# Pairing the TensorE bursts and state updates of a Mamba2 block: products of two units in one piece

## The chip, the cores and the metric

The kernel runs on one core of one Trainium2 chip. The metric is the device time of one launch in microseconds (us); lower is better. All data is float32. The four compute engines run their own instruction streams side by side: TensorE (PE, with its weight loads listed apart as PEld), VectorE (DVE), ScalarE (ACT) and GpSimd (POOL). The SP queue issues most of the DMAs. [...]

## The reference

One adaptive-layer-norm block over 4 sequences of 512 tokens with 512 features. A layer norm, scaled and shifted by values that come from a conditioning vector, goes through a Mamba2 mixer and is added back with a gate; then a second such layer norm goes through one matrix of signs (times a row mean) with a bias, again with a gate. The part that the change touches is the chunked scan of the mixer:

```python
    Y_diag = jnp.einsum('bcshn,bczhn,bhcsz,bczhp->bcshp', Cm, Bm, Lm, X)
    decay_states = jnp.exp(A_cum[..., -1:] - A_cum)
    states = jnp.einsum('bcshn,bhcs,bcshp->bchpn', Bm, decay_states, X)
    ...
    new_states = jnp.einsum('bhzc,bchpn->bzhpn', decay_chunk, states)
    states = new_states[:, :-1]
    state_decay_out = jnp.exp(A_cum)
    Y_off = jnp.einsum('bcshn,bchpn,bhcs->bcshp', Cm, states, state_decay_out)
```

There are 64 heads with 16 values each, in 8 groups that share B and C with 64 state entries, and chunks of 128 tokens. `Y_diag` needs, for each group, the product of B and C over the state entries (128 x 128, masked and multiplied by the decays of each head). `Y_off` needs the product of C with the state that came in from the chunk before. The new state is the old one, decayed, plus a product of B with the decayed inputs.

## The kernel before

The 2048 tokens are worked in 8 halves of 256 tokens (`NHALF`), two to a sequence, and each half in 2 chunks of 128. A **unit** is one chunk and one pair of groups: (h, c, gp) with gp from 0 to 3, so there are 8 x 2 x 4 = 64 units. For each half a "front" makes the layer norm, the projections (`pp_B`, `pp_C`, `pp_x`, `pp_z`, line 433), the convolution on ACT and DVE (lines 446 and 450), the turned copies (`pt_bt`, `pt_xt`) and the sums of the time steps. Behind each chunk come three "tails": the output projection (`po`, line 722), the second layer norm (`ph`, line 740) and the last matrix (`pf`, line 758).

The order is written by hand. Lists (`FIRST`, `SECOND`, `FRONT`, lines 770 to 793) give each piece of a front a step; the loop from line 828 runs the steps from -1. Step s runs the pieces due at s, then `burst`, then `stage2` of unit s, then `stage0` and `stage1` of unit s + 2. This text order is the priority: a compile-time scheduler places each engine's instructions by it as soon as they look ready and a buffer is free, so a piece that is held up lets later ones pass. `glued` (line 208) keeps products of one piece next to each other on TensorE.

- `burst(old, new)` (lines 594 to 608) issues up to four products into one PSUM tile `gy` with one buffer [...]: the state outputs of unit s (C times state, two products, one for each half of the rows) and the B times C products of unit s + 2 (again two). These are 64 rows deep, so the two of a pair lie on different halves of the array. Units of the first chunk of a sequence have no state coming in, and their bursts lack the first pair.
- `stage1` reads B times C out of `gy` on DVE, masked, into `gm` (line 619), runs 16 exponentials on ACT in place over `decay` tiles that a DMA has filled with broadcast sums (line 545), and multiplies both with two DVE instructions (line 623).
- `stage2` multiplies the decays with the inputs on TensorE into `py` (two glued pieces of eight products, output 32 partitions wide, lines 647 to 655), reads the state output from `gy` on DVE (line 664), adds `py` (669), and on POOL adds `xs` and multiplies by `z` (670, 673). Then, except in the last chunk of a sequence, it makes the new state of its pair of groups: POOL makes `xd` (line 680, two buffers), TensorE two products into a PSUM tile `pst` (line 685, 64 columns wide), POOL decays the old state into the new tile (line 690), and DVE adds `pst` (line 695); in the first chunk DVE copies `pst` instead (line 688). `pst` is one of the tiles of the tag `mm`, which has five buffers [...] and also serves all projections, turns and tails.

TensorE's products in float32 appear as two matmul records each in the trace. So a full burst has 8 records, `pst` of one unit 4, `py` of one unit 32.

Of the kernel before, what the change touches and what calls it, by code (L numbers as in the profile page):

```python
# [11 lines left out]
F32 = mybir.dt.float32  # L12
AF = mybir.ActivationFunctionType
ALU = mybir.AluOpType
AX = mybir.AxisListType
PSUM = bass.MemoryType.PSUM
P = 128

B, L, DM = 4, 512, 512
DI, NS, NG, NH = 1024, 64, 8, 64  # L20
HD = DI // NH
# [4 lines left out]
CH = 128  # L26
T = 256
NHALF = B * L // T
HPB = L // T
# [10 lines left out]
def adaln_mamba_block(  # L40
# [15 lines left out]
    nc = tc.nc  # L56
    mm = nc.tensor.matmul

    def bc(ap, n):

        return ap.unsqueeze(2).to_broadcast([ap.shape[0], ap.shape[1], n])

    def bc_mid(ap, n):

        return ap.unsqueeze(1).to_broadcast([ap.shape[0], n, ap.shape[1]])
# [3 lines left out]
    ps = ctx.enter_context(tc.tile_pool(name="ps", bufs=5, space=PSUM))  # L69
    wk = ctx.enter_context(tc.tile_pool(name="wk", bufs=2))  # L70
# [22 lines left out]
    upto = keep.tile([P, P], F32, name="upto")  # L93
# [114 lines left out]
    def glued(products, after=None):  # L208

        with tc.issue_after(after) if after else nullcontext():  # L210
            first = products[0]()  # L211
        with tc.issue_after(first.ins), tc.high_priority(offset=1000):
            for product in products[1:]:
                product()  # L214
# [89 lines left out]
    H = [dict(B={}, C={}, xt={}, xs={}, bt={}, z={}) for _ in range(NHALF)]  # L304
# [217 lines left out]
    NP = NG // 2  # L522
    HPP = 2 * HPG
    states = {}
    U0, U1, G = {}, {}, {}
    n_decay = [0]

    def is_first(h, c):
        return h % HPB == 0 and c == 0
# [10 lines left out]
    def exps(h, c, gp, ets):  # L540
        hd0 = c * NH + gp * HPP
        for r in range(2):
            for i in range(HPG):
                hd = hd0 + r * HPG + i
                nc.scalar.activation(  # L545
                    ets[r][:, i, :], ets[r][:, i, :], AF.Exp, bias=H[h]["st"][:, hd : hd + 1], scale=-1.0
                )
# [18 lines left out]
    def stage0(h, c, gp):  # L566

        n = f"{h}_{c}_{gp}"
        ets = AHEAD.get((h, c, gp))
        if ets is None:  # L570
            ets = own_decays()
            load_sums(h, c, gp, ets)
        e = None
        if not is_first(h, c):
            e = wk.tile([P, 2, CH], F32, tag="e", name=f"e_{n}")
            for r in range(2):
                lo = (2 * gp + r) * HPG
                nc.sync.dma_start(
                    e[:, r, :],
                    e_d[h, c, lo : lo + HPG, :].unsqueeze(1).to_broadcast([HPG, HD, CH]),  # L580
                )
        U0[h, c, gp] = (ets, e)

    def by_rows(gy, slot, h, c, gp, stationary):

        return [
            partial(
                mm, gy[:, r, slot, :], stationary[part],
                H[h]["C"][gp // 2][part, gp % 2, c * CH : (c + 1) * CH], start=True, stop=True,
            )  # L590
            for r, part in enumerate((slice(0, NS), slice(NS, P)))
        ]

    def burst(old, new):

        gy = ps.tile([P, 2, 4, CH], F32, tag="gy", bufs=1, name="gy_" + "_".join(map(str, old or new)))
        products = []
        if old is not None:
            h, c, gp = old
            k = (h % HPB) * 2 + c  # L600
            if k > 0:
                products += by_rows(gy, 1, h, c, gp, states[h // HPB, k][:, gp, :])
                G[old, 1] = gy
        if new is not None:
            h, c, gp = new
            products += by_rows(gy, 0, h, c, gp, H[h]["B"][gp // 2][:, gp % 2, c * CH : (c + 1) * CH])
            G[new, 0] = gy
        glued(products)

    def stage1(h, c, gp):  # L610

        n = f"{h}_{c}_{gp}"
        ets, e = U0.pop((h, c, gp))
        gm = wk.tile([P, 2, CH], F32, tag="gm", name=f"gm_{n}", bufs=3)
        nc.vector.tensor_mul(gm, G.pop(((h, c, gp), 0))[:, :, 0, :], bc_mid(upto, 2))
        if (h, c, gp) not in AHEAD:  # L620
            exps(h, c, gp, ets)
        for r in range(2):
            nc.vector.scalar_tensor_tensor(  # L623
                ets[r], ets[r], 1.0, bc_mid(gm[:, r, :], HPG), ALU.min, ALU.mult
            )
        U1[h, c, gp] = (ets, e)

    def stage2(h, c, gp):

        n = f"{h}_{c}_{gp}"
        k = (h % HPB) * 2 + c
        b = h // HPB
        ets, e = U1.pop((h, c, gp))
        hd0 = c * NH + gp * HPP
        xp = H[h]["xt"][gp][:, c, :]
        xg = xp.rearrange("p (j q e) -> p j q e", q=4, e=HD)[:, :, 0:4:3, :]

        def by_head(v):

            return v.rearrange("p (j q) -> p j q", q=2).unsqueeze(3).to_broadcast([P, HPG, 2, HD])

        py = ps.tile([P, 2, CH], F32, tag="y", bufs=1, name=f"py_{n}")

        for r in range(2):
            glued([
                partial(
                    mm, py[32 * j : 32 * j + 32, r, :],  # L650
                    xp[:, r * 2 * P + 32 * (2 * j + q) : r * 2 * P + 32 * (2 * j + q) + 32],
                    ets[r][:, 2 * j + q, :], start=(q == 0), stop=(q == 1),
                )
                for q in range(2) for j in range(HPG // 2)
            ], H[1]["last"] if (h, c) == (0, 1) else None)

        cs = slice(c * CH, (c + 1) * CH)
        zg = H[h]["z"][gp][:, :, cs]
        xs = H[h]["xs"][gp][:, :, cs]
        t = wk.tile([P, 2, CH], F32, tag="gm", name=f"yt_{n}", bufs=3)  # L660

        ew = nc.vector if h == NHALF - 1 and c == 1 and gp >= NP // 2 else nc.gpsimd
        if k > 0:
            nc.vector.tensor_mul(t, G.pop(((h, c, gp), 1))[:, :, 1, :], e)
            if ew is nc.vector:
                ew.tensor_add(t, t, xs)
                ew.tensor_add(t, py, t)
            else:
                nc.vector.tensor_add(t, py, t)  # L669
                ew.tensor_add(t, t, xs)  # L670
        else:
            nc.vector.tensor_add(t, py, xs)  # L672
        ew.tensor_mul(zg, t, zg)  # L673

        if k < HPB * 2 - 1:
            if gp == 0:
                states[b, k + 1] = wk.tile([P, NP, P], F32, tag="S", name=f"S_{b}_{k + 1}")
            new = states[b, k + 1][:, gp, :]
            xd = wk.tile([P, HPG, 2, HD], F32, tag="xd", name=f"xd_{n}")
            nc.gpsimd.tensor_tensor(xd, xg, by_head(H[h]["ed"][:, hd0 : hd0 + HPP]), ALU.mult)  # L680
            xd2 = xd.rearrange("p j q e -> p (j q e)")
            pst = ps.tile([P, P], F32, tag="mm", name=f"pst_{n}")
            bt = H[h]["bt"][gp // 2][:, c, gp % 2, :]
            for r in range(2):
                mm(pst[r * NS : (r + 1) * NS, :], bt[:, r * NS : (r + 1) * NS], xd2[:, r * P : (r + 1) * P],  # L685
                   start=True, stop=True)
            if k == 0:
                nc.vector.tensor_copy(new, pst)
            else:
                nc.gpsimd.tensor_tensor(  # L690
                    new.rearrange("p (h e) -> p h e", e=HD),
                    states[b, k][:, gp, :].rearrange("p (h e) -> p h e", e=HD),
                    bc(H[h]["dec"][:, c * NP + gp, :], HD), ALU.mult,
                )
                nc.vector.tensor_add(new, new, pst)


    gates = {}
# [124 lines left out]
    h = NHALF - 1  # L823
# [3 lines left out]
    units = [(h, c, gp) for h in range(NHALF) for c in range(2) for gp in range(NP)]  # L827
    for step in range(-1, max(steps) + 1):
        for f, args in steps.get(step, []):
            f(*args)  # L830

        new = units[step + 2 : step + 3] if step >= 0 else units[0:2]
        if step < 0:
            for unit in new:
                burst(None, unit)
                stage0(*unit)
                stage1(*unit)
        elif step < len(units):
            if new or not is_first(*units[step][:2]):
                burst(units[step], new[0] if new else None)  # L840
            stage2(*units[step])
            for unit in POST.get(step, []):
                ahead(*unit)
            for unit in new:
                stage0(*unit)
                stage1(*unit)
# [42 lines left out]
```

## Time and profile before

| what | value |
|---|---|
| median of 3 runs | 748.45 us (746.47 to 752.62) |
| the profiled execution | 747.6 us |
| its span, first to last instruction | 745.9 us |
| TensorE busy | 711.2 us, 5196 matmul records |
| VectorE busy | 602.6 us, 1218 instructions |
| ScalarE busy | 523.7 us, 1507 instructions |
| GpSimd busy | 260.4 us, 313 instructions |
| `gy` matmul records | 448, of them 192 of states |
| `pst` matmul records | 192 |
| `py` matmul records | 2048 |

Times within the trace count from the first instruction. Matmuls are pipelined: the time that one record is said to take (about 0.27 us for a moving side of 128) is much longer than the time from its start to the start of the next, so the cost of a piece on TensorE is read from start to start, and a busy TensorE isn't one at its peak. In the group rows a name such as `gy<-C,S` says which tile is written from which; `128*64` behind a matmul is the part of the array it uses, rows times columns.

### The profile page before, as it was taken

The numbers are of one execution on the slowest core, as the hardware profiler recorded it, in microseconds if no ns is written. First come the engines' busy times: TensorE is split into PE (matmuls) and PEld (weight loads), VectorE is DVE, ScalarE is ACT, GpSimd is POOL, SyncE is SP. The second block draws the span as 40 slices with busy tenths as digits, with TensorE's granted clock in tenths as the row PEclk, the third lists the DMA queues.
The fourth block names the chain that finished last, engine by engine and source line by source line (L and its number), as shares of the span: only waits on it lengthen the run. The fifth ranks groups of instructions, "written<-read, shape, count | busy, mean of one in ns | idle before, by whom it ended". The sixth has DMA issues, their size and how long they took to land.

```text
span 745.9 us, 15107 instructions
## 1 busy us (share of the span) xinstructions
PE 711.2 (95%) x5196; PEld 503.2 (67%) x5196; DVE 602.6 (81%) x1218; ACT 523.7 (70%) x1507; POOL 260.4 (35%) x313
## 2 busy tenths in 40 slices
PE   6999979899999999999999999999999999999997
PEld 3787647566677666686667666876667866677654
DVE  3968889866999579986899769996699867997795
ACT  2476668648796596775877777764969658798941
POOL 4021325334242433353224243533324232343452
PEclk9999989899999999999999999999999999999999
DMA  8991865435654266434634246543544436458610
GB/s 280 317 289 39 237 164 121 113 86 138 125 146 125 63 158 140 106 101 99 158 101 119 75 108 165 149 110 69 139 125 121 129 79 175 104 152 167 143 58 28
DMA packets 119068, 99.25 MB, mean 133 GB/s; under 512 B 73984, under 2 KB 97152, under 8 KB 118992
## 3 DMA queue, kind: packets, MB, share of 16 engines
q1 hardware_dynamic: 117808, 96.39, 50.6%
q0 software_dynamic: 896, 1.38, 0.6%
q8 instruction: 41, 0.67, 0.4%
q10 hardware_dynamic: 288, 0.52, 0.2%
q14 instruction: 35, 0.29, 0.1%
HBM read 92.47 MB, written 5.79 MB: 132 GB/s over the span
## 4 chain that ended last, share of the span: by engine, by line
PE 77%; ACT 14%; DVE 5%; issue 2%; DMA 2%; ACTq 0%; POOL 0%; SPq 0%; DVEq 0%
PE pp_x L433 16%; PE po L722 15%; PE pp_z L433 12%; ACT decay L545 10%; PE pp_B L433 7%; PE pp_C L433 7%; PE pf L758 4%; PE py L211 3%; PE py L214 3%; PE gy L211 2%; PE pt_xt L463 2%; PE pst L685 2%; PE pa L367 1%; DMA decay<-sums_d 1%; ACT h L742 1%
## 5 line engine op out<-in xcount | busy, mean ns | idle before, releaser
L545 ACT ACTIVATE decay<-decay,st 128x128 f32<-128x128 f32 x960 | 293.0, 395 | 4.0 <-DMA decay<-sums_d 3.7
L623 DVE SCALAR_TENSOR_TENSOR decay<-decay,gm 128x1024 f32<-128x1024 f32 x120 | 156.8, 1308 | 25.1 <-ACT decay L545 24.1
L433 PE MATMUL pp_x<-hT,win 128*128 128x259 f32 x512 | 122.5, 394 | 5.8 <-ACT decay L545 5.8
L433 PE MATMUL pp_z<-hT,win 128*128 128x256 f32 x512 | 118.1, 383 | 0.0
L433 PEld LDWEIGHTS pp_x<-hT,win 128*128 128x128 f32 x512 | 98.0, 195 | 24.1 <-ACT decay L545 6.0
L722 PE MATMUL po<-wout,z 128*128 128x512 f32 x256 | 113.9, 595 | 0.0
L433 PEld LDWEIGHTS pp_z<-hT,win 128*128 128x128 f32 x512 | 94.3, 189 | 16.1 <-issue 3.3
L680 POOL TENSOR_TENSOR xd<-xpad,st 128x256 f32<-128x256 f32 x48 | 37.6, 784 | 188.3 <-PE pst L685 143.0
L450 DVE SCALAR_TENSOR_TENSOR u_x<-pp_x,cw,u_x 128x256 f32<-128x256 f32 x192 | 82.9, 473 | 1.4 <-ACT u_x L446 0.5
L722 PEld LDWEIGHTS po<-wout,z 128*128 128x128 f32 x256 | 47.4, 190 | 52.6 <-issue 51.7
L512 ACT ACTIVATE uz<-pp_z,zb 128x256 f32<-128x256 f32 x64 | 26.8, 468 | 62.3 <-PE pp_z L433 62.3
L670 POOL TENSOR_TENSOR yt<-yt,xs 128x256 f32<-128x256 f32 x46 | 41.1, 893 | 84.4 <-DVE yt L669 84.4
L214 PE MATMUL py<-decay,xpad 128*32 128x128 f32 x1680 | 67.4, 276 | 0.0
L673 POOL TENSOR_TENSOR z<-yt,z 128x256 f32<-128x256 f32 x62 | 58.5, 944 | 17.1 <-DVE yt L672 13.6
L433 PE MATMUL pp_B<-hT,win 128*128 128x259 f32 x256 | 60.9, 388 | 0.9 <-ACT st L426 0.9
L758 PE MATMUL pf<-bwT,h 128*128 128x512 f32 (+1 forms) x136 | 59.1, 575 | 0.8 <-ACT h L742 0.6
L433 PE MATMUL pp_C<-hT,win 128*128 128x259 f32 x256 | 59.0, 382 | 0.0
L503 POOL TENSOR_TENSOR xs<-u_x,rr 128x512 f32<-128x512 f32 x32 | 42.1, 1318 | 40.8 <-DVE u_x L455 40.8
L433 PEld LDWEIGHTS pp_B<-hT,win 128*128 128x128 f32 x256 | 47.0, 189 | 10.8 <-ACT st L426 1.7
L433 PEld LDWEIGHTS pp_C<-hT,win 128*128 128x128 f32 x256 | 47.8, 189 | 7.8 <-DVE u_B L450 0.3
L446 ACT ACTIVATE u_x<-pp_x,cb,cw 128x256 f32<-128x256 f32 x64 | 35.2, 559 | 25.1 <-PE pp_x L433 24.8
L211 PE MATMUL py<-decay,xpad 128*32 128x128 f32 x240 | 47.5, 280 | 3.8 <-ACT decay L545 2.8
(155 smaller groups left out, 1134.0 us busy)
## 6 DMA issues: line engine op xcount, KB each, us to landing
decay<-sums_d SPq DMA_DIRECT2D x120, 256.0 KB
decay<-sums_d SPq DMA_DIRECT2D x120, 128.0 KB
rr<-r_d SPq DMA_DIRECT2D x64, 128.0 KB
e<-e_d SPq DMA_DIRECT2D x96, 64.0 KB
win<-in_w_inT SPq DMA_DIRECT2D x4, 1024.0 KB
xr<-in_x SPq DMA_DIRECT2D x16, 256.0 KB
res<-o SPq DMA_DIRECT2D x15, 256.0 KB
x<-in_x SPq DMA_DIRECT2D x14, 256.0 KB
```

The lines of the kernel that those rows point to most:

```text
L211: first = products[0]()
L214: product()
L433: last = mm(pm, win[:, k, col : col + P], H[h]["hT"][:, k, lo:], start=(k == 0), stop=(k == NK - 1))
L450: nc.vector.scalar_tensor_tensor(u[:, j, :], pm[:, k : k + T], cw[:, t, k : k + 1], u[:, j, :], ALU.mult, ALU.add)
L503: nc.gpsimd.tensor_tensor(xs, xc, rr, ALU.mult)
L545: nc.scalar.activation(ets[r][:, i, :], ets[r][:, i, :], AF.Exp, bias=H[h]["st"][:, hd : hd + 1], scale=-1.0)
L623: nc.vector.scalar_tensor_tensor(ets[r], ets[r], 1.0, bc_mid(gm[:, r, :], HPG), ALU.min, ALU.mult)
L670: ew.tensor_add(t, t, xs)
L673: ew.tensor_mul(zg, t, zg)
L680: nc.gpsimd.tensor_tensor(xd, xg, by_head(H[h]["ed"][:, hd0 : hd0 + HPP]), ALU.mult)
L722: last_po = mm(po, H[h]["z"][g // 2][:, g % 2, c * CH : (c + 1) * CH], wout[:, g, :], start=(g == 0), stop=(g == NKI - 1))
L758: mm(pf, h2[:, k, :], bwT[:, k, cols], start=(k == 0), stop=(k == NK - 1))
```

## The change

`burst` now takes lists of units. It is called in even steps only, and makes the state outputs of units s and s + 1 and the B times C products of units s + 2 and s + 3: eight glued products into one `gy` tile, whose four slots are now all used. The tile keeps its size and its one buffer. The readers on DVE stay as they were, one read for each unit.

The new states move out of `stage2` into `new_states`, called in the second unit of each pair of units (odd gp). `xd` is still made by POOL for each unit, in its own step. The four products of both units are glued and go to one `pst` tile of 128 x 256; the decay on POOL and the add (or copy) on DVE become one instruction of 128 x 256 for two of 128 x 128.

```diff
     def burst(old, new):
-        gy = ps.tile([P, 2, 4, CH], F32, tag="gy", bufs=1, name="gy_" + "_".join(map(str, old or new)))
+        gy = ps.tile([P, 2, 4, CH], F32, tag="gy", bufs=1, name="gy_" + "_".join(map(str, (old or new)[0])))
         products = []
-        if old is not None:
-            h, c, gp = old
+        for i, (h, c, gp) in enumerate(old):
             k = (h % HPB) * 2 + c
             if k > 0:
-                products += by_rows(gy, 1, h, c, gp, states[h // HPB, k][:, gp, :])
-                G[old, 1] = gy
-        if new is not None:
-            h, c, gp = new
-            products += by_rows(gy, 0, h, c, gp, H[h]["B"][gp // 2][:, gp % 2, c * CH : (c + 1) * CH])
-            G[new, 0] = gy
+                products += by_rows(gy, 2 + i, h, c, gp, states[h // HPB, k][:, gp, :])
+                G[(h, c, gp), 1] = gy[:, :, 2 + i, :]
+        for i, (h, c, gp) in enumerate(new):
+            products += by_rows(gy, i, h, c, gp, H[h]["B"][gp // 2][:, gp % 2, c * CH : (c + 1) * CH])
+            G[(h, c, gp), 0] = gy[:, :, i, :]
         glued(products)
...
             xd = wk.tile([P, HPG, 2, HD], F32, tag="xd", name=f"xd_{n}")
             nc.gpsimd.tensor_tensor(xd, xg, by_head(H[h]["ed"][:, hd0 : hd0 + HPP]), ALU.mult)
-            xd2 = xd.rearrange("p j q e -> p (j q e)")
-            pst = ps.tile([P, P], F32, tag="mm", name=f"pst_{n}")
-            bt = H[h]["bt"][gp // 2][:, c, gp % 2, :]
-            for r in range(2):
-                mm(pst[r * NS : (r + 1) * NS, :], bt[:, r * NS : (r + 1) * NS], xd2[:, r * P : (r + 1) * P],
-                   start=True, stop=True)
...
+            XD[gp % 2] = xd.rearrange("p j q e -> p (j q e)")
+            if gp % 2:
+                new_states(h, c, gp - 1)
+
+    def new_states(h, c, gp):
...
+        both = slice(gp, gp + 2)
+        new = states[b, k + 1][:, both, :].rearrange("p g e -> p (g e)")
+        pst = ps.tile([P, 2, P], F32, tag="mm", name=f"pst_{h}_{c}_{gp}")
+        bt = H[h]["bt"][gp // 2]
+        glued([
+            partial(
+                mm, pst[r * NS : (r + 1) * NS, i, :], bt[:, c, i, r * NS : (r + 1) * NS],
+                XD[i][:, r * P : (r + 1) * P], start=True, stop=True,
+            )
+            for i in (1, 0) for r in range(2)
+        ])
+        pst = pst.rearrange("p g e -> p (g e)")
+        if k == 0:
+            nc.vector.tensor_copy(new, pst)
+        else:
+            nc.gpsimd.tensor_tensor(
+                new.rearrange("p (h e) -> p h e", e=HD),
+                states[b, k][:, both, :].rearrange("p g (h e) -> p (g h) e", e=HD),
+                bc(H[h]["dec"][:, c * NP + gp : c * NP + gp + 2, :].rearrange("p j h -> p (j h)"), HD), ALU.mult,
+            )
+            nc.vector.tensor_add(new, new, pst)
...
         if step < 0:
+            burst([], new)
             for unit in new:
-                burst(None, unit)
                 stage0(*unit)
                 stage1(*unit)
         elif step < len(units):
-            if new or not is_first(*units[step][:2]):
-                burst(units[step], new[0] if new else None)
+            if step % 2 == 0 and (step + 2 < len(units) or not is_first(*units[step][:2])):
+                burst(units[step : step + 2], units[step + 2 : step + 4])
             stage2(*units[step])
```

More of the change, by code (lines that the diff above doesn't have):

```diff
@@ L618, in stage1 @@
         gm = wk.tile([P, 2, CH], F32, tag="gm", name=f"gm_{n}", bufs=3)
-        nc.vector.tensor_mul(gm, G.pop(((h, c, gp), 0))[:, :, 0, :], bc_mid(upto, 2))
+        nc.vector.tensor_mul(gm, G.pop(((h, c, gp), 0)), bc_mid(upto, 2))
         if (h, c, gp) not in AHEAD:
@@ L663, in stage2 @@
         if k > 0:
-            nc.vector.tensor_mul(t, G.pop(((h, c, gp), 1))[:, :, 1, :], e)
+            nc.vector.tensor_mul(t, G.pop(((h, c, gp), 1)), e)
             if ew is nc.vector:
@@ L675, in stage2 @@
         if k < HPB * 2 - 1:
-            if gp == 0:
-                states[b, k + 1] = wk.tile([P, NP, P], F32, tag="S", name=f"S_{b}_{k + 1}")
-            new = states[b, k + 1][:, gp, :]
             xd = wk.tile([P, HPG, 2, HD], F32, tag="xd", name=f"xd_{n}")
             nc.gpsimd.tensor_tensor(xd, xg, by_head(H[h]["ed"][:, hd0 : hd0 + HPP]), ALU.mult)
-            xd2 = xd.rearrange("p j q e -> p (j q e)")
-            pst = ps.tile([P, P], F32, tag="mm", name=f"pst_{n}")
-            bt = H[h]["bt"][gp // 2][:, c, gp % 2, :]
@@ L684, in stage2 @@
-            for r in range(2):
-                mm(pst[r * NS : (r + 1) * NS, :], bt[:, r * NS : (r + 1) * NS], xd2[:, r * P : (r + 1) * P],
-                   start=True, stop=True)
[L687 to L695, printed above, removed]
+            XD[gp % 2] = xd.rearrange("p j q e -> p (j q e)")
@@ new lines, in stage2 @@
+            if gp % 2:
+                new_states(h, c, gp - 1)
+    XD = {}
+    def new_states(h, c, gp):
+        k = (h % HPB) * 2 + c
+        b = h // HPB
+        if gp == 0:
+            states[b, k + 1] = wk.tile([P, NP, P], F32, tag="S", name=f"S_{b}_{k + 1}")
+        both = slice(gp, gp + 2)
[19 more added lines that the diff above has]
+            nc.vector.tensor_add(new, new, pst)
```

## The prediction, made before the change was run

> **What bounds the kernel now.** I read the page's engine table and chain first, then a table by stretches, then TensorE's timeline. The page's lines of busy time and of the chain that ended last:
>
> ```profile
> PE 711.2 (95%) x5196; PEld 503.2 (67%) x5196; DVE 602.6 (81%) x1218; ACT 523.7 (70%) x1507; POOL 260.4 (35%) x313
> ...
> PE 77%; ACT 14%; DVE 5%; issue 2%; DMA 2%; ACTq 0%; POOL 0%; SPq 0%; DVEq 0%
> ```
>
> TensorE is the bound, but 23% of the chain runs elsewhere. The table by stretches (busy PE, PEld, DVE, ACT, POOL, then clock and DMA) shows where, for one half of steady state and for a stretch in it:
>
> ```profile
> 326.00:414.00 88.00, 86.50 (x642) 62.09 (x643) 72.44 (x150) 63.66 (x185) 31.48 (x38) 1.00 0.48 117
> ```
> ```profile
> 346.00:360.00 14.00, 13.21 (x127) 8.77 (x125) 9.37 (x15) 13.46 (x43) 4.17 (x4) 1.00 0.52 111
> ```
>
> Over the half TensorE idles 1.5 us of 88. From 346 to 360 ACT is full (13.46 of 14), and the chain goes through its exponentials. So what TensorE sheds counts nearly everywhere, but not there. What a piece costs is read from start to start in TensorE's timeline:
>
> ```profile
> 352.47 3.68 PE L758 MATMUL pf<-bwT,h 128*128 128x512 f32 x8
> 356.09 0.37 PE L211 MATMUL gy<-C,S 64*128 64x128 f32 x1
> ...
> 356.30 0.27 PE L211 MATMUL gy<-C,S 64*128 64x128 f32 x1
> ...
> 356.41 0.39 PE L214 MATMUL gy<-C,B 64*128 64x128 f32 x4
> 356.73 0.30 PE L211 MATMUL py<-decay,xpad 128*32 128x128 f32 x1
> ...
> 357.74 0.44 PE L685 MATMUL pst<-xd,bt 128*64 128x128 f32 x4
> 358.11 1.09 PE L329 MATMUL phT<-ident,x 128*128 128x128 f32 x8
> ```
>
> A full burst takes 356.73 - 356.09 = 0.64 us, although its later pairs of records follow each other at 0.11 (356.30 to 356.41). The first step is 0.21 instead of 0.11, and the exit, from the last start to the next piece's start, 0.20 instead of 0.11. `pst` takes 358.11 - 357.74 = 0.37.
>
> [...] at each change of `64*128`, `128*32`, `128*64` and `128*128` about 0.1 us is lost, and about another 0.1 behind the first loads of a burst. [...] the state add of 128x128 takes 270 ns, an add of 128x256 413, [...]
>
> **The change part by part.**
>
> Bursts. Before there are 2 in step -1, one in each of the steps 0 to 61 and two at the end: 66. After there are 1, 31 and 1: 33. The products are the same; 33 pieces are merged into others. What two more products cost in a running burst comes from a burst that has only two:
>
> ```profile
> 38.54 0.37 PE L211 MATMUL gy<-C,B 64*128 64x128 f32 x1
> ...
> 38.96 3.77 PE L433 MATMUL pp_B<-hT,win 128*128 128x259 f32 x16
> ```
>
> It takes 38.96 - 38.54 = 0.42, so two more products cost 0.64 - 0.42 = 0.22. A merged burst takes 0.64 + 2 x 0.22 = 1.08 against 2 x 0.64 = 1.28: 0.20 saved. The way into it isn't saved where `py` follows, since `py` is another mode as well:
>
> ```profile
> 311.60 3.70 PE L758 MATMUL pf<-bwT,h 128*128 128x512 f32 x8 [0.16 <-ACT xpad L489]
> 315.23 0.30 PE L211 MATMUL py<-decay,xpad 128*32 128x128 f32 x1
> ```
>
> `pf` to `py` takes 3.63, `pf` to `gy` 3.62 (352.47 to 356.09). So bursts: 33 x 0.20 = 6.6 us.
>
> New states. 48 pieces of 0.37 become 24 of twice the records. The nearest row for a longer piece in the same mode `128*64` is `pa`:
>
> ```profile
> 361.32 0.66 PE L367 MATMUL pa<-hT,win 128*64 128x128 f32 x8
> 361.91 0.30 PE L211 MATMUL py<-decay,xpad 128*32 128x128 f32 x1
> ```
>
> Eight records take 0.59, so a pair saves 2 x 0.37 - 0.59 = 0.15, and 24 save 3.6 us. On TensorE together: 10.2 us.
>
> DVE and POOL, from the groups by shape:
>
> ```profile
> L690 POOL TENSOR_TENSOR S<-S,st 128x128 f32<-128x128 f32 x32 | 24.6, 775 | 28.5 <-PE gy L214 15.5 <-DVE S L688 9.8 <-DVE S L695 3.2
> L669 DVE TENSOR_TENSOR yt<-py,yt 128x256 f32<-128x256 f32 x46 | 19.0, 413 | 1.4 <-PE py L214 1.3
> L695 DVE TENSOR_TENSOR S<-S,pst 128x128 f32<-128x128 f32 x32 | 8.7, 270 | 0.0
> L688 DVE COPY S<-pst 128x128 f32<-128x128 f32 x16 | 4.4, 277 | 0.1
> ```
>
> With 413 ns for 128x256, adds save 8.7 - 16 x 0.413 = 2.1 and copies 4.4 - 8 x 0.413 = 1.1: 3.2 us on DVE, of which the chain's DVE share (5%) lets about 0.2 through. POOL's 16 larger decays, at 0.9 each (the POOL add of that shape, 893 ns), take 14.4 for 24.6. POOL is 35% busy and 0% of the chain: nothing. If its idle time were gone, it would be worth up to 10 us.
>
> Moved steps and waits, each taken at nothing. Half the state outputs and B times C are made a step earlier; B and C tiles are shared by both units of a pair, and the states were added three steps before. The state of an even unit is ready a step later; its reader is still three steps off, and the bursts between 340 and 363 show three steps lasting 22 us. With that cover gone, the burst would wait for DVE's add, and `py` and the projections behind it. The one `gy` buffer still waits for the same last two DVE reads, of the step before. A merged burst delays `py` by 0.44 in even steps and frees 0.64 in odd ones; DVE's reads are late by the same and DVE has queued work. No DMA is added or moved past another in the text. `pst` waits for the second `xd`, bounded in the rivals. A scheduler that places instructions by readiness may reorder elsewhere: bounds of 7 us either way, the price of one stall below; I take zero.
>
> Sum: 10.2 x 0.77 (the chain's share of TensorE) + 0.2 = 8.1 us. The profiled execution took 747.6 (span 745.9 and 1.7 around it): 739.5 us, with a span of 737.8. That run lies 0.85 below the median of 748.45; I keep 739.5. About 1% (7.5 us) is what a measurement of this kernel can tell from no change, so "faster" means below 741.0.
>
> **The rivals.**
>
> A, likeliest: as summed. Half-full realization to all of it (5 to 10.2 us): 737 to 743.
>
> B, most of it is swallowed: ACT (full for 14 us in each half of 88) and DVE set the pace at the joints, and TensorE only waits longer there. For it: in that stretch alone lie two of a half's eight bursts, and in the first 150 us, with 10 of the 66 bursts, TensorE is busy only 130. Against it: TensorE's idle of 1.5 us per half. With 30% realized: 744.5; its range is 743 to 748.
>
> C, slower: the paired `pst` waits for POOL. Both `xd` buffers are now held until one piece has read them, [...]. The wait view speaks to it:
>
> ```profile
> POOL xd L680 <- PE pst L685: 143.0, 26, 10.4
> ```
>
> POOL now waits for TensorE and not the reverse: `xd` runs as soon as its buffer is freed, a step or more ahead. After the change one `pst` frees both buffers, and both `xd` (622 ns median) can run a step ahead again. If the scheduler instead puts the second `xd` behind its unit's `xs` (1.3 us) and `z` (0.9), 24 pairs wait up to 2.2 us: 53 us. It decides from 8.1 / 24 = 0.34 us per pair on. I give a few pairs: 749 to 762, with 756 as its value (16.5 us lost in waits, 0.7 a pair).
>
> D, an early stall goes or comes. There are two, at 98.30 and 133.6:
>
> ```profile
> 98.30 5.44 PE L433 MATMUL pp_x<-hT,win 128*128 128x259 f32 x16 [5.77 <-ACT decay L545]
> ```
>
> Idle of 5.77, and then the slow clock: 5.44 for what takes 3.67 elsewhere (`pp_C` at 367.48: 16 records in 3.67), 1.8 more, so 7.5 us. The second, `pst` waiting 3.2 us behind `xpad`, costs about 5.8 likewise (its `pp_x` takes 6.25). 24 fewer `mm` tiles make it likelier that one goes: 732.
>
> **How the numbers follow.** A 0.58, B 0.25, C 0.10, D 0.07. A lies below 741 in 0.49 of its 0.58; with D faster is 0.56. B, the rest of A and 0.02 of C (749 to 756) make the same 0.36; slower (above 755.9) is 0.08. The predicted time is A's, 739.5. The range runs from 731 (D's time less 1; 0.04 below it) to 749 (B's end and the noise; 0.10 above it). A's own range is 737 to 743.
>
> **What would show it.** Right: `gy` in 33 pieces of up to 16 records with about 1.08 us from start to start, `pst` in 24 of 8 with 0.59, TensorE's busy time some 8 to 10 us lower, adds on DVE at 16 x 0.41. Wrong in the realization: the same prices, but more TensorE idle behind ACT and DVE in the stretches where ACT is full. C: waits of `pst` for `xd`. The prediction is also wrong if a merged burst takes 1.28, that is, if the loss lies with each product and not with the piece, or if a new gap of over 3 us with a lower clock stands in the first 150 us.

## The result, and the profile after

The changed kernel takes 753.18 us (median of 12 runs, 751.5 to 755.04), the kernel before 748.28 beside it (12 runs): a ratio of 1.0063, 95% interval 1.0045 to 1.0081. The forecast of 739.5, with its range up to 749, was wrong: a gain of some 8 us was forecast, and the kernel is 4.9 us slower. The profiled execution took 751.99 us with a span of 750.3, against 745.9.

The engine line and the chain of the page after:

```profile
PE 700.3 (93%) x5196; PEld 502.0 (67%) x5196; DVE 605.4 (81%) x1194; ACT 521.0 (69%) x1507; POOL 248.9 (33%) x297
...
PE 52%; DVE 23%; ACT 12%; issue 5%; POOL 3%; DMA 3%; SPq 0%; DVEq 0%; ACTq 0%; POOLq 0%
```

TensorE is busy 10.9 us less, as the prices said, and yet the span is 4.4 longer: TensorE now stands still more. In the chain its share fell from 77% to 52%, and VectorE's rose from 5% to 23%.

**The prices.** A merged burst and a paired `pst` in TensorE's timeline after:

```profile
200.68 0.37 PE L211 MATMUL gy<-C,S 64*128 64x128 f32 x1
...
201.22 0.61 PE L214 MATMUL gy<-C,B 64*128 64x128 f32 x8
201.77 0.30 PE L211 MATMUL py<-decay,xpad 128*32 128x128 f32 x1
...
438.75 0.32 PE L211 MATMUL pst<-xd,bt 128*64 128x128 f32 x1
...
439.34 3.72 PE L433 MATMUL pp_z<-hT,win 128*128 128x256 f32 x16
```

The burst takes 201.77 - 200.68 = 1.09 (1.08 forecast), `pst` 439.34 - 438.75 = 0.59 (0.59 forecast). The readers, from the groups by shape:

```profile
L703 POOL TENSOR_TENSOR S<-S,st 128x256 f32<-128x256 f32 x16 | 14.3, 896 | 0.0
L708 DVE TENSOR_TENSOR S<-S,pst 128x256 f32<-128x256 f32 x16 | 6.6, 411 | 0.4
L701 DVE COPY S<-pst 128x256 f32<-128x256 f32 x8 | 3.3, 417 | 0.3
```

These too are what was forecast (0.9, 413 and 413).

**Where the time went.** TensorE's rows of the waits view (us in total, times, longest), before and after:

```profile
PE pp_x L433 <- ACT decay L545: 5.8, 1, 5.8
...
PE py L211 <- ACT decay L545: 2.8, 3, 0.9
...
PE gy L211 <- DVE gm L619: 0.5, 1, 0.5
```
```profile
PE pt_bt L463 <- DVE u_x L450: 8.1, 5, 2.3
PE pp_x L433 <- DVE u_C L450: 6.1, 1, 6.1
...
PE py L211 <- ACT decay L545: 3.7, 3, 1.2
PE gy L211 <- DVE gm L617: 3.0, 3, 1.0
```

All TensorE rows add up to 31.2 us before and 46.3 after: 15.1 more. With 10.9 less busy that is 4.2, the span's 4.4. The largest new row is `pt_bt` behind VectorE's `u_x`, which the view before doesn't have. It comes in every second half, so TensorE's timeline at that place, before and then after, shows it whole:

```profile
210.35 0.34 PE L423 MATMUL pn<-dq,ones 128*64 128x64 f32 x4
210.73 0.63 PE L463 MATMUL pt_bt<-ident,B 128*128 128x128 f32 x4
...
214.03 3.78 PE L433 MATMUL pp_B<-hT,win 128*128 128x259 f32 x16 [0.29 <-ACT st L426]
217.64 0.60 PE L463 MATMUL pt_xt<-ident,u_x 128*128 128x128 f32 x4
```
```profile
210.21 0.34 PE L423 MATMUL pn<-dq,ones 128*64 128x64 f32 x4
...
213.87 0.63 PE L463 MATMUL pt_bt<-ident,B 128*128 128x128 f32 x4 [2.32 <-DVE u_x L450]
215.04 1.09 PE L753 MATMUL ph<-ident,t 128*128 128x128 f32 x4 [0.55 <-DVE u_x L450]
215.93 4.61 PE L433 MATMUL pp_B<-hT,win 128*128 128x259 f32 x16
220.37 0.60 PE L463 MATMUL pt_xt<-ident,u_x 128*128 128x128 f32 x4
```

At `pn` the changed kernel is 0.14 ahead; at `pt_xt` it is 2.73 behind. Two waits make 2.87, and `pp_B` behind them runs slower (4.44 from start to start for 3.61). The two waits come again at 392.75 and 570.34 (2.3 and 0.55), but there `pp_B` takes 3.51: the slowing is no fixed part of the loss. `pt_bt` takes an `mm` buffer, and the one that it waits for is held by a `pp_x` that VectorE has yet to read. VectorE's timeline there, before and after:

```profile
204.67 0.41 DVE L664 TENSOR_TENSOR yt<-gy,e 128x256 f32<-128x256 f32 x1
...
207.55 0.44 DVE L450 SCALAR_TENSOR_TENSOR u_x<-pp_x,cw,u_x 128x256 f32<-128x256 f32 x1
...
209.32 1.26 DVE L450 SCALAR_TENSOR_TENSOR u_x<-pp_x,cw,u_x 128x256 f32<-128x256 f32 x3
210.50 1.41 DVE L623 SCALAR_TENSOR_TENSOR decay<-decay,gm 128x1024 f32<-128x1024 f32 x1
```
```profile
206.16 0.41 DVE L662 TENSOR_TENSOR yt<-gy,e 128x256 f32<-128x256 f32 x1
...
209.04 0.45 DVE L450 SCALAR_TENSOR_TENSOR u_x<-pp_x,cw,u_x 128x256 f32<-128x256 f32 x1
...
211.21 2.13 DVE L621 SCALAR_TENSOR_TENSOR decay<-decay,gm 128x1024 f32<-128x1024 f32 x1
213.25 1.64 DVE L450 SCALAR_TENSOR_TENSOR u_x<-pp_x,cw,u_x 128x256 f32<-128x256 f32 x4
```

VectorE is 1.49 us late, and a multiply of 2.13 us now stands ahead of the reads that free the buffer. The four reads of `u_x` follow behind it at 213.25, 2.04 us after its start. The lateness begins 20 us earlier, at the time-step chain. VectorE and then ScalarE there, after:

```profile
187.74 0.28 DVE L370 TENSOR_SCALAR dl<-pa 128x128 f32<-128x128 f32 x1
190.69 1.23 DVE L621 SCALAR_TENSOR_TENSOR decay<-decay,gm 128x1024 f32<-128x1024 f32 x1 [2.67 <-ACT decay L545]
```
```profile
188.05 0.28 ACT L371 ACTIVATE du<-pa 128x128 f32<-128x128 f32 x1 [2.52 <-DVE dl L370]
188.22 2.14 ACT L545 ACTIVATE decay<-decay,st 128x128 f32<-128x128 f32 x7
```

And ScalarE before:

```profile
185.61 2.44 ACT L545 ACTIVATE decay<-decay,st 128x128 f32<-128x128 f32 x8 [0.60 <-DMA decay<-sums_d]
187.96 0.26 ACT L371 ACTIVATE du<-pa 128x128 f32<-128x128 f32 x1
```

Before, the eight exponentials ran ahead of `du`, and VectorE had no wait ahead of its multiply. After, `du` stands ahead of them and waits for VectorE's `dl`; the exponentials come 2.6 us later, and VectorE idles 2.67. Nothing in the diff touches these lines: the scheduler laid another order. SyncE's queue changed as well: stores of the result wait longer in it (line 775, 36.0 us in 6 waits, against 20.1 in 3), ahead of loads of decays: one such load leaves at 183.04, behind a store, for 180.76 before.

So the first theory was a chain: changed order on ScalarE and SyncE, VectorE late, a projection's buffer freed late, TensorE waits and at times is slowed. Its rivals: the one `gy` tile is held longer; `gm` buffers are short; VectorE's pace swallows whatever TensorE gains, in any order.

### The profile page after: what moved, and what is told of

Read it like the earlier page. It is cut to its first block, busy times and chain, and to the rows that moved or that the text cites. A ratio compares the mean times of both kernels' runs of the same rounds, so it can differ in the third digit from the quotient of the medians.

```text
span 750.3 us, 15030 instructions
## 1 busy us (share of the span) xinstructions
PE 700.3 (93%) x5196; PEld 502.0 (67%) x5196; DVE 605.4 (81%) x1194; ACT 521.0 (69%) x1507; POOL 248.9 (33%) x297
## 4 chain that ended last, share of the span: by engine, by line
PE 52%; DVE 23%; ACT 12%; issue 5%; POOL 3%; DMA 3%; SPq 0%; DVEq 0%; ACTq 0%; POOLq 0%
PE pp_z L433 12%; PE pp_x L433 10%; ACT decay L545 8%; PE po L735 7%; PE pf L771 5%; DVE decay L621 5%; PE pp_B L433 4%; PE pp_C L433 3%; DVE u_B L450 2%; DMA decay<-sums_d 2%; PE py L211 2%; PE py L214 2%; PE pt_xt L463 2%; DVE u_C L450 2%; DVE u_x L450 2%
## 5 line engine op out<-in xcount | busy, mean ns | idle before, releaser
L621 DVE SCALAR_TENSOR_TENSOR decay<-decay,gm 128x1024 f32<-128x1024 f32 x120 | 156.8, 1309 | 34.3 <-ACT decay L545 33.6
L668 POOL TENSOR_TENSOR yt<-yt,xs 128x256 f32<-128x256 f32 x46 | 44.8, 974 | 127.0 <-DVE yt L667 97.0
L671 POOL TENSOR_TENSOR z<-yt,z 128x256 f32<-128x256 f32 x62 | 55.6, 896 | 81.0 <-DVE yt L670 68.6
L450 DVE SCALAR_TENSOR_TENSOR u_x<-pp_x,cw,u_x 128x256 f32<-128x256 f32 x192 | 81.0, 472 | 0.4 <-ACT u_x L446 0.3
L675 POOL TENSOR_TENSOR xd<-xpad,st 128x256 f32<-128x256 f32 x48 | 33.7, 719 | 63.2 <-PE pst L214 36.7
L214 PEld LDWEIGHTS py<-decay,xpad 128*32 128x32 f32 x1680 | 47.4, 109 | 0.0
```

The costliest lines, as they stand in the source:

```text
L450: nc.vector.scalar_tensor_tensor(u[:, j, :], pm[:, k : k + T], cw[:, t, k : k + 1], u[:, j, :], ALU.mult, ALU.add)
L621: nc.vector.scalar_tensor_tensor(ets[r], ets[r], 1.0, bc_mid(gm[:, r, :], HPG), ALU.min, ALU.mult)
```

## The experiments

The expectations use names for theories of their own; the text beside each says which is meant. "Before" is the kernel before on the same chip.

**Either part alone.** `bursts_only` is the changed kernel with the old lines of the new states back in `stage2`; `states_only` is the kernel before with the new ones (`new_states`).

> Only the bursts are paired, the new states are made unit by unit as before. Theory 1 (the pieces got cheaper as priced, but the changed order leaves ScalarE waiting before the time-step chain, VectorE late and TensorE standing before a turned copy, some 4 us three times): here the compiled order keeps eight exponentials ahead of the absolute value, as before, so no such stall: 33 x 0.20 = 6.6 us less TensorE work shows for the most part, 742 to 744 us. Theory 2 (ScalarE and VectorE are co-bounds and swallow any TensorE saving): 747 to 749. Theory 3 (the paired burst itself hurts, since the first unit of the pair waits longer for its products): above 751.

> Only the new states are paired, the bursts stay one for each unit. Theory 1: the compiled order puts the absolute value ahead of the exponentials in the odd halves (3, 5, 7) but keeps the exponentials first in the even ones, where the long stalls lay, so most of 24 x 0.15 = 3.6 us shows: 744 to 747. Theory 2: 748. A theory 4 (the paired state piece in the middle of the time-step product is what delays that product and all behind it): 751 to 753, nearly as slow as the whole change.

Measured: bursts alone 752.16 (ratio 1.0035, 1.0011 to 1.0058), states alone 747.85 (0.9992, 0.9981 to 1.0002), before 748.33. The loss comes with the bursts, though not in every run (746.48 to 754.15 for the bursts alone, with the slowest run profiled, so its figures may be high). From one `phT` to the one two halves later, in halves 2 to 6, before takes 176.7 and 175.7 us, states alone 175.2 both times, bursts alone 179.1 and 177.8, both 178.9 and 177.6. So in steady state the states give about what they were priced at (6 of 24 pieces, 6 x 0.15 = 0.9 a pair of halves), while the bursts, priced at 8 x 0.20 = 1.6 less, take 2.3 more. The bursts alone lose although ScalarE kept the order of before at the time-step chain:

```profile
187.77 2.45 ACT L545 ACTIVATE decay<-decay,st 128x128 f32<-128x128 f32 x8
190.13 0.26 ACT L371 ACTIVATE du<-pa 128x128 f32<-128x128 f32 x1
```

So the order of `du` can't be the whole of it; the range of 751 and over was named for theory 3, in which the paired burst itself hurts.

**The order at the time-step chain.** `act_first` is the whole change with the two first readers of the time steps exchanged:

```diff
-        nc.vector.tensor_scalar(relu, pa, 0.0, None, ALU.max)
         nc.scalar.activation(u, pa, AF.Abs)
+        nc.vector.tensor_scalar(relu, pa, 0.0, None, ALU.max)
```

`exps_first` is the whole change with an ordering edge that puts `du` behind the first exponentials of the unit at hand:

```diff
-        nc.scalar.activation(u, pa, AF.Abs)
+        with tc.issue_after(first_exps[0]) if h > 1 else nullcontext():
+            nc.scalar.activation(u, pa, AF.Abs)
```

`loads_first` is the whole change with the store of the result and the load of `xr` queued on SyncE behind decay loads already issued; `before_loads_first` does the same to the kernel before:

```diff
-        nc.sync.dma_start(xr, x[h * T + c * CH : h * T + (c + 1) * CH, :])
+        with tc.issue_after(last_load[0]):
+            nc.sync.dma_start(xr, x[h * T + c * CH : h * T + (c + 1) * CH, :])
...
-            nc.sync.dma_start(out[h * T + c * CH : h * T + (c + 1) * CH, cols], o)
+            stores.append((out[h * T + c * CH : h * T + (c + 1) * CH, cols], o))
```

> The whole change, with the two readers of the time-step product swapped: ScalarE's absolute value first, VectorE's maximum second, so that ScalarE no longer waits for VectorE's queue. Theory 1: the wait of ScalarE there shrinks from 2.5 us to about 1.2 in each of six halves, VectorE is less late, and the three stalls before the turned copy shrink or go: 745 to 750. Theory 2 and 3: no change, 752 to 754.

> The whole change, with one edge of order more: ScalarE issues the absolute value only behind the eight exponentials that were ahead of it before the change. Theory 1: the three long stalls of TensorE before the turned copy go and the time falls to 738 to 743 us, below the kernel before. Theory 2: 752 to 754, as without the edge. If the stalls go but others come in their place: 745 to 751.

> The whole change; in the queue of loads (SP) the store of a finished output block and the load of a residual block stand only behind the decay loads that the text has issued by then. Theory 5: in the slow order the store, which waits for VectorE's last add, stands ahead of a decay load; that load leaves at 183.0 instead of 180.8, the exponentials start 2.5 us later, VectorE idles 2.7 us in the stretch of each even half where it is otherwise full, and TensorE then stands 2.4 us [...]. With the loads ahead, the wait of VectorE before its first decay product at 187.9 shrinks to under 1 us and the time falls to 738 to 745 us. Theory 2 (VectorE's work itself is the bound in that stretch and any order costs the same): 751 to 754.

> The kernel before with the same edges of order in the queue of loads, as a control. Theory 5: before the change the decay load already left ahead of the store, so nothing to win: 746 to 750. If the edges help both kernels alike (below 744), they say nothing about the change.

Measured: `act_first` 749.84 (1.0020, 1.0008 to 1.0031), `exps_first` 760.98 (1.0166, 1.0131 to 1.0201), `loads_first` 756.85 (1.0102, 1.0073 to 1.0131), its control 748.99 (1.0003, 0.9991 to 1.0015). The exchange won back 3.4 of the 4.9 us, in the range of theory 1, and TensorE's waits of `pt_bt` for `u_x` fell from 8.1 to 2.2 us. The exponentials start hardly earlier in it (188.00 for 188.22), but `du` starts sooner (187.48 for 188.05), and VectorE works on the time steps where it idled. The edge gave ScalarE the order of before, but the decays' load itself was late, and ScalarE still idled:

```profile
187.66 2.44 ACT L548 ACTIVATE decay<-decay,st 128x128 f32<-128x128 f32 x8 [2.26 <-DMA decay<-sums_d]
```

With the loads ahead, VectorE's idle at that place shrank to 1.29, but waits of TensorE came in the other halves. So the chain above is what happens in the changed kernel, and the exchange eases it; but to force the order of `du` or of the loads back made the kernel slower, and neither order is shown to be the cause by itself.

**Less work in the time-step chain.** `short_after` and `short_before` leave out four of the eight terms of the logarithm's series (VectorE, 282 ns each).

```diff
-SERIES = [1.0 / k for k in range(17, 1, -2)]
+SERIES = [1.0 / k for k in range(9, 1, -2)]
```

> The whole change with four terms of the series for the logarithm left out (of eight), so 4 x 0.28 = 1.1 us less VectorE work in the time-step chain of each half, at the head of the stretch where VectorE is full. Theory 6 (in that stretch VectorE is the bound, so that TensorE's savings there don't show): 1.1 us or more less in each of the six later halves, [...]: 740 to 746. If TensorE is the bound throughout: no change, 752 to 754.

> The kernel before with the same four terms of the series left out. Theory 6: before the change TensorE and VectorE end that stretch together (TensorE stands 0.36 us there), so less VectorE work alone brings at most 6 x 0.4 = 2.4 us: 745 to 748. If VectorE was the bound before as well: 741 to 743.

Measured: 741.59 (0.9899, 0.9876 to 0.9923) and 747.97 (0.9996, 0.9981 to 1.0011). At first sight VectorE's work is the cause: half a series is worth 11.6 us after and nothing before. The trace says otherwise. Of the 9.6 us between the two profiled spans, 7.6 were won ahead of half 2, around the two early stalls of the prediction's rival D. TensorE at the first of them in the changed kernel, and with the short series:

```profile
98.58 5.31 PE L433 MATMUL pp_x<-hT,win 128*128 128x259 f32 x16 [6.05 <-DVE u_C L450]
```
```profile
93.81 1.99 PE L433 MATMUL pp_x<-hT,win 128*128 128x259 f32 x8 [0.52 <-DVE u_C L450]
97.56 1.99 PE L433 MATMUL pp_x<-hT,win 128*128 128x259 f32 x8 [1.76 <-DVE u_C L450]
```

The next `pp_B` starts 3.3 us earlier (110.61 for 113.86), and the first `pf`, behind the second stall, 7.9 (136.91 for 144.81). Half 2 begins at 173.9 for 181.5; from there on two pairs of halves take 176.6 and 179.0, together 0.9 less than in the full change (178.9, 177.6). In `short_before` the first stall shrank too (2.73 for 5.77), and half 2 began no earlier (181.5 for 181.4). So the early part can change by some 8 us with the order, by luck as far as these runs tell, and a shorter stall alone doesn't bring it; on the steady state this experiment settled nothing.

**Buffers.** `early_reads` reads all of the paired `gy` behind the burst, so that the second unit doesn't hold it (`gm` with four buffers); `four_gm` came last and only gives `gm` four buffers for three, `before_four_gm` is its control.

```diff
         glued(products)
+        for h, c, gp in new:
+            gm = wk.tile([P, 2, CH], F32, tag="gm", name=f"gm_{h}_{c}_{gp}", bufs=4)
+            nc.vector.tensor_mul(gm, G.pop(((h, c, gp), 0)), bc_mid(upto, 2))
+            READ[(h, c, gp), 0] = gm
+        for h, c, gp in old:
+            if (h % HPB) * 2 + c > 0:
+                t = wk.tile([P, 2, CH], F32, tag="gm", name=f"yt_{h}_{c}_{gp}", bufs=4)
+                nc.vector.tensor_mul(t, G.pop(((h, c, gp), 1)), U1[h, c, gp][1])
+                READ[(h, c, gp), 1] = t
```

> The whole change, but VectorE reads all four parts of the paired burst's gy in one go right behind the burst (B times C of units s+2 and s+3 into gm, the state outputs of s and s+1 times their decays into yt), in place of a read in each unit's own stage; the tag gm has four buffers for three (1 KB more). Nothing is left out. Theory A, the one gy tile is held by the second unit's late reads, so that the next burst waits (py to gy 1.18 us a pair, 7.7 us at gy for VectorE's gm in all): the wait at gy falls under 1.5 us in all, a pair of halves takes 176 to 177 us against 178.9 and 177.6, and the time is 746 to 749. Theory B, what was lost lies in VectorE's order around the time-step chain (the stall ahead of pt_bt): gy's wait may fall, but a pair of halves stays at 178 us or more and the time at 751 to 755. Rival C, two more VectorE reads ahead of py's only delay the multiplies that TensorE waits for: over 756.

> The whole change, with four buffers for three under the tag gm (masked products and yt; 1 KB more). Nothing is left out. Theory E: two state outputs now lie ready together, and VectorE's reads of gy wait for a gm buffer until POOL's multiply has let go of an older yt (9.4 us in 11 waits after, 3.1 in 4 before; 1.43 of them right ahead of the time-step chain in every second half). Then these waits fall below 3 us, the wait ahead of pt_bt below 1 us, and the time is 745 to 749. Rival B, the orders make the waits and this is one of several: POOL's waits fall, others come, 750 to 756.

> The kernel before with four buffers under the tag gm. Nothing is left out. The control for the buffer: theory E expects 746 to 748.5, since there is little to mend (3.1 us of waits for POOL's z on VectorE). Rival B: anything from 745 to 753, as another order comes out.

Measured: `early_reads` 758.3 (1.0125, 1.0102 to 1.0148), `four_gm` 753.28 (1.0068, 1.0044 to 1.0093), its control 749.58 (1.0008, 0.9995 to 1.0022). With early reads TensorE waits at `gy` nearly as long as in the full change (1.9 behind `gm` and 0.8 behind `yt`, for 3.0), and its rows add up to 49.5. The time is in the range of rival C. Since the wait stayed, this doesn't tell what a free tile would be worth; what speaks against the held tile is that only 3.0 of TensorE's 46.3 us of waits in the full change lie there. With four buffers VectorE's waits for POOL's multiply fell from 9.4 us to 1.9, and the time didn't move; what grew are the waits for exponentials, 40.1 us for 33.6:

```profile
DVE decay L621 <- ACT decay L545: 40.1, 38, 3.1
```

The short buffer fell: when its waits went, others took their place.

**The exchange with either part, and with none.** The exchange of `act_first` in three more kernels.

> The paired bursts alone (states as before), with the two first readers of the time steps exchanged: ScalarE's absolute value is traced ahead of VectorE's maximum. Nothing is left out. Theory B, the loss of the paired bursts is a queue order that the scheduler happens to give around the time-step chain, and any nudge of that order can undo it: the time falls from 752 to 747 to 750, as it fell from 753 to 750 with both parts. Theory A, the held gy tile: the exchange does nothing for it, 751 to 754.

> The paired states alone (bursts as before), with the same exchange of the two first readers. Nothing is left out. Theory B: the paired states had no loss to undo, so their gain of 24 x 0.15 = 3.6 us at most can show only in part: 745 to 748, and it may beat the kernel before by up to 0.4%. Rival: the exchange moves the stalls for the worse here, 749 to 753.

> The kernel before with the same exchange alone. Nothing is left out. It tells what the exchange is worth without the pairing. If it mends what the pairing broke, it does nothing here: 747.5 to 749. If it is a gain of its own: 743 to 746, and the pairing's loss stands as it was. If it is a lottery of orders: anything from 744 to 753.

Measured, before 748.64: bursts 750.51 (1.0028, 1.0014 to 1.0042), states 744.33 (0.9929, 0.9904 to 0.9954), none 749.86 (1.0012, 1.0000 to 1.0023). By itself the exchange is no gain. Against the exchanged kernel before, the states are worth 5.5 us, the bursts cost 0.7 (the two intervals overlap), and both together (`act_first`, 749.84 on another chip) stand level. The states with the exchange are the fastest full kernel of the study, 4.3 us under before. But in the profiles 3.0 us of their lead over the exchanged kernel before lie ahead of half 2, and only 1.2 in halves 2 to 6, where 1.8 were priced. Their chain is TensorE's nearly as before:

```profile
PE 72%; ACT 11%; DVE 6%; issue 4%; DMA 4%; POOL 2%; SPq 0%; ACTq 0%; DVEq 0%; POOLq 0%
```

**VectorE relieved.** Four kernels (before, after, either part) without one of the convolution's three taps on VectorE, that is without 128 instructions of 0.47 us.

```diff
-            for k in range(KS - 1):
+            for k in range(1, KS - 1):
                 nc.vector.scalar_tensor_tensor(
```

> The kernel before with one of the convolution's three taps on VectorE left out (the fourth tap is ScalarE's): 128 instructions of 0.47 us, 60 us of VectorE's 603. It is the base for the three light kernels beside it. If VectorE's pace sets the stretches from phT to pt_bt (28 us of VectorE's work in some 29 to 32), the kernel gets faster by 8 to 20 us: 728 to 740. If TensorE alone sets the time, 744 to 748.

> The whole change with the same tap of the convolution left out. Theory D, the pairing's 10.2 us on TensorE were lost because VectorE paces the stretches: with VectorE relieved they come back, and this is 6 to 10 us faster than the light kernel before. Theory B, the loss comes from the orders that the scheduler lays out and the waits that these make, whatever VectorE's load: the light pair differs by -3 to +5 us, as the full one does (+4.9). The wait ahead of pt_bt (2.5 us in every second half) would be gone under D, and stay or move under B.

> The paired bursts alone with the same tap left out. Theory D: 4 to 7 us under the light kernel before (33 x 0.20 = 6.6 us on TensorE). Theory B: between 2 us under and 5 us over it.

> The paired states alone with the same tap left out. Theory D: 2 to 4 us under the light kernel before (24 x 0.15 = 3.6 us). Theory B: within 3 us of it on either side.

| version | median us, full | TensorE busy | TensorE waits | median us, light | TensorE busy | TensorE waits |
|---|---|---|---|---|---|---|
| before | 748.28 | 711.2 | 31.2 | 737.60 | 706.6 | 24.6 |
| bursts alone | 752.16 | 708.9 | 39.2 | 735.63 | 702.0 | 26.7 |
| states alone | 747.85 | 705.4 | 35.8 | 730.76 | 702.4 | 22.2 |
| both | 753.18 | 700.3 | 46.3 | 738.25 | 698.0 | 35.6 |

The ratios of the light ones to the full kernel before are 0.9862 (0.9835 to 0.9889), 0.9835 (0.9810 to 0.9860), 0.9765 (0.9739 to 0.9791) and 0.9864 (0.9833 to 0.9895). Waits are all TensorE rows of the waits view; busy and waits together follow the spans within 1.1 us. Relieved, the bursts turn from +3.8 to -2.0 and the states from -0.5 to -6.8. In halves 2 to 6 alone the profiles show the bursts at +4.5 us in the full kernel and -0.5 in the light one (-3.2 priced), the states at -2.0 and -3.0 (-1.8 priced), and both at +4.1 and +3.1. So the bursts alone lost in the steady state with VectorE's full load and not without; the states had their price there all along, and their 6.8 is more than the price and partly luck of the early part (1.8 ahead of half 2). Both together win nothing (+0.65): that is in theory B's range, as the bursts' -2.0 is at its edge, while the states' -6.8 lies outside both theories. The wait of `pt_bt` is gone, and others stand in its place in the light changed kernel:

```profile
PE pst L211 <- DVE u_x L450: 4.0, 3, 1.8
PE pa L367 <- ACT hT L346: 3.8, 4, 1.1
PE py L211 <- ACT decay L545: 3.7, 3, 1.2
PE pp_B L433 <- ACT u_x L446: 3.3, 3, 1.1
```

The light kernels also have orders of their own, so that a difference of a few us between two of them isn't pace alone, and how much of the change for the bursts is VectorE's load and how much a new order isn't shown.

## Why the prediction was wrong, point by point

- **Prices and sum on TensorE**: right. 33 bursts of 1.09 and 24 `pst` of 0.59; busy time fell by 10.9 for 10.2 forecast.
- **VectorE and POOL**: the durations right. The 24 instructions saved 3.2 us of adds and copies (8.7 and 4.4 to 6.6 and 3.3), yet VectorE's busy time went from 602.6 to 605.4: other instructions took longer in their new places, the two rows of line 299 (a layer norm's scaling) 6.0 us more. Of these 32, 18 now overlap a POOL instruction, for 2 before (mean 0.88 us against 0.55 for the rest).
- **The share of 0.77**: wrong. The chain before says what TensorE's work was worth in the orders of before. In the new ones TensorE held 52% of it, and gained time turned into waits.
- **"Moved steps and waits, each taken at nothing"**: this is the step that failed, in its last term, "may reorder elsewhere: bounds of 7 us either way ... I take zero". The span came out at 750.3 for 737.8, 12.5 over where the bound was 7. Behind it stand 15.1 us of new waits on TensorE, many of 0.5 to 2.3 and not one stall; orders did change (`du`, the stores), but how much of the 15.1 is order and how much VectorE's pace stays open. "DVE's reads are late by the same and DVE has queued work" was the cover, and it cut the other way: queued work, at `pt_bt` a multiply of 2.13 us, is what stood ahead of the read that TensorE needed. In the stretch from `phT` to `pt_bt` (181.4 to 210.7 before) VectorE is busy 27.3 of 29.3 us, so 2.0 us of idle time were all it had to catch up 1.5.
- **"The one gy buffer still waits for the same last two DVE reads"**: not quite, but small: 3.0 us of waits for 0.5. `early_reads` didn't remove them, so their worth is bounded by their size alone.
- **Rival B** (swallowed by ACT and DVE) had the kind right: the same prices, more idle behind both. Its size of 743 to 748 left no room for a loss.
- **Rival C**: not seen. `pst` has no wait for `xd`, and POOL's own wait for `pst` went from 143.0 to 36.7 us. The measured 753.18 lies in its range of 749 to 762, but by luck: its mechanism isn't there.
- **Rival D**: the first early stall stayed (6.05 for 5.77). Its price of 7.5 isn't confirmed: where it nearly went, in `short_after`, 3.3 us were won by the next `pp_B` and the rest of the 7.6 around the second stall; and where it halved, in `short_before`, nothing was.

What is shown: the prices; that the loss comes with the bursts (3.8 us in the orders as first compiled, 0.7 with the exchange); that it isn't there for the bursts alone with VectorE relieved (5.8 us of difference, order included); and that forcing back the order of `du` or of the loads, or a fourth `gm` buffer, doesn't undo it. What stays open: which cause made it, VectorE's pace or the orders; why the two parts together lose even with VectorE relieved, and why the scheduler chose these orders; the trace shows an order, not its reasons. To keep all the other queues as they were before while only TensorE's pieces are merged wasn't tried.

## What to carry to other kernels

A price per piece, read from start to start, can be right to the hundredth and still say nothing of the end time, when a second engine fills 27 of 29 us in the stretches between: cost the new waits on that engine as a term of its own, with both signs. Where a compile-time scheduler lays the queues, any edit is also a new order, here worth from 3 us less (`act_first`) to 8 more (`exps_first`) than the changed kernel; so try each part alone and each with a harmless exchange before judging it. Here the states gave their small price in the steady halves (2.0 us for 1.8), though alone they don't show in the time (747.85 for 748.33); the bursts, with nearly twice their price, lost. And look where a gain lies: the largest ones here, of `short_after` and of the states with the exchange, came by half or more ahead of half 2.

## What the runs showed of the hardware

In the changed kernel `pp_B` ran slower after waits of 2.32 and 0.55 us with 0.6 us of work in between: 4.44 us for 3.61, with a granted clock of 0.50 from 214.4 to 217.8. The same clock of 0.50 stood behind the first early stall in both kernels: from 98.3 to 101.0 before, behind a wait of 5.77, and from 98.6 to 101.0 after, behind one of 6.05. In the changed kernel two halves after the slow `pp_B`:

```profile
392.75 0.63 PE L463 MATMUL pt_bt<-ident,B 128*128 128x128 f32 x4 [2.30 <-DVE u_x L450]
393.93 0.63 PE L753 MATMUL ph<-ident,t 128*128 128x128 f32 x4 [0.55 <-DVE u_x L450]
394.39 3.67 PE L433 MATMUL pp_B<-hT,win 128*128 128x259 f32 x16
```

Here, and again at 570.34, the same two waits left the clock at 1.00, and `pp_B` took 3.51 from start to start (to 397.90). So these two waits cost more than their length in one case of three here; what decides between them wasn't tried.

The same VectorE multiply of 128 x 1024 took 1.21 us at its fastest and 2.13 ahead of `pt_bt`, with the same mean over all 120 in both kernels (1308 and 1309 ns). POOL's timeline at the same place, after:

```profile
210.97 1.28 POOL L741 TENSOR_TENSOR xr<-xr,gates 128x512 f32<-128x512 f32 x1 [0.66 <-DVE t L299]
```

The multiply (211.21 to 213.34) overlaps it by 1.05 us, and so it is all three times that it takes 2.13 ahead of `pt_bt`. Over the two traces no multiply that overlaps no POOL instruction takes more than 1.23 us (59 before, 77 after), and each of those over 1.3 (32 and 15) overlaps one; yet the 13 that overlap only POOL's add of `xs` into `yt` aren't slower (1.21 to 1.23 us). So what POOL runs beside it goes with the length of a VectorE instruction; no run varied that alone.
